# A decoder layer on one core: scores for the maxima from three of six pairs of parts in two halves of TensorE's rows, and cq and most of the down projection as plain float32 products

## The chip, the cores and the metric

The kernel runs on one core of a Trainium2 chip. The core has a matrix engine (TensorE, PE in the profile, with its weight loads as PEld), three engines for element-wise work (VectorE or DVE, ScalarE or ACT, GpSimd or POOL), a queue that issues DMAs (SyncE, SP), on-chip memory of 128 partitions (SBUF), and eight accumulator banks that TensorE writes (PSUM). The metric is the device time of one execution in microseconds; the time of a kernel is the median of its runs.

## The reference

One pre-norm decoder layer on 64 sequences of 128 tokens with 256 features, all in float32:

```python
x = x + attn(layernorm(x), W_attn, b_attn, W_proj, b_proj, bias_table)  # 16 heads of 16, causal, T5 bias
x = x + xattn(layernorm(x), ctx, ctx, mask, Wq, Wk, Wv, Wo)             # 16 heads of 16, keys masked
x = x + ffn(layernorm(x), w_gate, w_up, w_down)                         # 256 -> 704 -> 256
```

Attention is softmax(q k / 4 + bias) v. In the feed-forward part, both operands of each of the three products are first rounded, block by block of 16 values, to a 4-bit floating grid and scaled back; `h = silu(gate) * up`, rounded again, is multiplied by the rounded `w_down`. The rounding makes the result sensitive to small errors, so the products before it are made at float32 accuracy.

## The kernel before

Two sequences make a group; 32 groups go through the layer. Every step of a group has a name, such as `a0.sa2` (self-attention, sequence 0 of the group, second product of scores for heads 8 to 11) or `f1.dn` (feed-forward, sequence 1, down projection). `a` is self-attention, `c` cross-attention, `d` and `f` are the layer norms ahead of cross-attention and feed-forward. A list written out by hand, `ORDER`, gives every step a place and a stage. The steps of a group with stage s are issued s rounds of the list later, so that parts of six or seven groups are interleaved, and each engine works through its own instructions in that order. `SETUP` places the preparation of weights and bias tables among the first groups' steps, `BANKS` says which of the eight PSUM banks a step uses, `BUFS` how many buffers a tile name has.

How float32 accuracy is had from TensorE:

- *Split products* (`dense`, float32r operands): an operand is held as a high part (ScalarE, `high`) and the rest (VectorE, `low`). Three matmuls, high x high, high x low, low x high, make one product.
- *Plain products* (`plain`, float32 operands): one matmul, which appears in the trace as two passes.
- *Three bfloat16 parts*: queries and keys are cut into three parts (`Heads.part`, `take`, `rest`, `mid`, `low`). They are stored to DRAM (`store`) and loaded back (`Attention.load`) with rows = (part, dimension) and heads side by side, so that 96 rows hold six pairs of parts: q's parts (0,1,2), (0,1), (0) against k's parts in reverse order.

Attention for one sequence: `scores` (`sa`) makes q k for four heads at a time, a matmul of 96 rows each, `maxima` (`mx`, VectorE) adds bias or mask and takes each row's maximum, `tm`, `tw`, `tl` transpose the negated maxima and cut them into two bfloat16 parts, `bc` (`spread_max`) writes these by two DMAs into rows 96 and 97 of the loaded queries, whose partner rows in the keys hold ones. `scores_t` (`sb`) makes the transposed scores from 98 rows, so that the maximum is already subtracted; `ex` takes the exponential, `ph` and `pl` cut it into two float16 parts, `av` multiplies with the values, `cb`, `rv`, `cm` sum and normalise, `yt`, `yh`, `po`, `ad` project and add to x.

`cq` (queries of cross-attention) is a split product from `Norm.T` of kind d, whose low half VectorE makes (`d.lo`, L379). The down projection (`Feed.down`, L734) has six blocks of the 704 hidden features: five of 128 as split products, 15 matmuls, and the last 64 with high and low in the two halves of one tile, `hE`, two matmuls. Its operand `hT` is copied from a transposition by ScalarE (`turn_high`) and its low half is made by VectorE (`turn_low`, L722, L726).

Loading (L518) issues three DMAs, of 48, 32 and 16 rows of 4 KB. On SP the order in one round is:

```
mg  c0.lk  a0.bc  c1.lk  cq.st0  ck.st0  c0.lq  ck.st1  a1.bc  cq.st1  out  xg  c1.lq  cg
c0.bc  aq.st0  aq.st1  c1.bc  ak.st0  ak.st1  a0.lq  a0.lk  a1.lk  a1.lq
```

Of the kernel before, what the change touches and what calls it, by code (L numbers as in the profile page):

```python
# [9 lines left out]
F32 = mybir.dt.float32  # L10
F32R = mybir.dt.float32r
# [7 lines left out]
P = 128  # L19
# [23 lines left out]
    f0.am1:5 a0.mx1:2 a0.sa3:2 c1.ph1:4 d.lo:3 f1.rd2:6 c0.rv1:4 c1.av0:4 a0.mx3:2 a.ln:1 a0.sa2:2 ck.p0:2  # L43
    c0.cm1:4 c0.yh0:4 mg:3 a0.mx2:2 cq.mm:3 a1.sa0:2 ck.n1:2 cq.p0:3 c1.rv0:4 c1.cb0:4 f0.am2:5 c1.pl1:4
    c0.yt1:4 c0.yh1:4 a0.tm:2 c1.cm0:4 c1.av1:4 f1.ml0:6 cq.n1:3 c0.po:4 c1.yt0:4 a0.tw:2 ck.p1:2 c1.cb1:4
    f0.am3:5 ck.n2:2 c1.rv1:4 a0.tl:2 cq.p1:3 c1.cm1:4 a1.sa1:2 c1.yt1:4 a1.mx0:2 a1.mx1:2 c1.yh0:4 c0.lk:3
    ck.p2:2 c1.yh1:4 cq.n2:3 cq.p2:3 c0.ad:4 a0.bc:2 c1.lk:3 a0.sd0:2 c1.po:4 c1.ad:4 a0.sd1:2 f1.ml1:6 cq.st0:3
    f1.t0:6 f1.hi0:6 f.bn:4 f.ag:4 ck.st0:2 nm:3 f.ep:4 f0.xn0:5 c0.lq:3 f0.rd0:5 a1.sa2:2 f1.t1:6 f1.hi1:6
    a0.sb0:2 a0.ex0:2 a0.sb1:2 a0.ex1:2 a1.sa3:2 f1.lo0:6 f1.g1:5 f.pow:4 a0.sd2:2 cv.mm:2 f0.rd1:5 a0.sb2:2
    ck.st1:2 f.sh:4 a0.ph0:2 f1.lo1:6 f.ln:4 a.tp:1 f1.g0:5 a1.mx2:2 cv.p0:2 a1.mx3:2 f0.rd2:5 a.hi:1 f1.th0:5  # L50
    x.am0:4 x.am1:4 a.lo:1 cv.n1:2 f1.gt0:5 a0.pl0:2 a0.sd3:2 a1.tm:2 f1.dn:6 a0.sb3:2 x.am4:4 a1.tw:2 f1.th1:5
    f0.ml0:5 cv.p1:2 x.am2:4 x.am3:4 x.xn0:4 a1.tl:2 f1.gt1:5 c0.sa0:3 a0.ex2:2 c0.sa1:3 f1.ad:6 cv.n2:2 f1.u0:5
    a0.ex3:2 f1.u1:5 f0.ml1:5 c0.mx0:3 c0.mx1:3 a1.sd0:2 a1.bc:2 a1.sb0:2 cq.st1:3 a1.sd1:2 f1.bo0:5 x.rd0:4
    f1.bo1:5 x.rd1:4 a1.sb1:2 f1.am0:5 c0.sa2:3 a0.ph1:2 cv.p2:2 a1.ex0:2 f0.t0:5 c0.sa3:3 c0.mx2:3 out:6
    aq.mm:1 xg:0 c0.mx3:3 a1.sd3:2 x.rd2:4 f1.am1:5 a1.ex1:2 a0.pl1:2 f0.hi0:5 a1.sd2:2 f0.lo0:5 aq.p0:1 c1.lq:3
    f1.am2:5 a1.sb3:2 a0.av0:2 f0.t1:5 f0.hi1:5 a1.sb2:2 f0.lo1:5 cg:1 c0.tm:3 a1.ph0:2 a0.cb0:2 a0.rv0:2 aq.r:1
    c0.tw:3 a1.ex2:2 a0.cm0:2 f0.dn:5 c0.tl:3 a0.av1:2 aq.p1:1 a0.cb1:2 c1.sa2:3 a0.rv1:2 c1.sa0:3 x.ml0:4
    a1.pl0:2 a0.yt0:2 a1.ex3:2 f0.ad:5 a0.cm1:2 a0.yh0:2 ak.mm:1 c1.mx0:3 a0.yt1:2 c1.sa3:3 c1.mx2:3 c0.bc:3
    c1.sa1:3 a1.av0:2 c1.mx3:3 c0.sb0:3 f1.am3:5 a1.ph1:2 x.ml1:4 c0.sb1:3 ak.p0:1 a1.rv0:2 f.tp:4 aq.p2:1
    ak.r:1 a0.yh1:2 c0.ex0:3 a0.po:2 c0.ex1:3 c0.sb2:3 f.hi:4 a1.pl1:2 c1.mx1:3 f.lo:4 a1.cb0:2 aq.st0:1 ak.p1:1  # L60
    c0.sb3:3 a1.av1:2 aq.st1:1 a1.cb1:2 c1.tm:3 a1.rv1:2 av.mm:1 c0.ph0:3 c1.tw:3 a1.cm0:2 c0.ex2:3 a1.cm1:2
    f1.xn0:5 c1.tl:3 c1.bc:3 ak.p2:1 c0.ex3:3 ak.st0:1 a1.yt0:2 a1.yh0:2 a1.yt1:2 a1.yh1:2 c0.ph1:3 a.bn:0
    f0.g0:4 a.ag:0 a1.po:2 a0.ad:2 av.p0:1 f1.rd0:5 f0.th0:4 f0.g1:4 a1.ad:2 ak.st1:1 av.n1:1 d.bn:2 f0.gt0:4
    a0.lq:1 c0.pl0:3 a0.lk:1 c0.av0:3 c0.cb0:3 av.p1:1 c1.sb0:3 c0.pl1:3 a1.lk:1 c1.sb1:3 av.n2:1 f0.th1:4
    d.ag:2 f0.u0:4 a1.lq:1 a.ep:0 d.ep:2 f1.rd1:5 d.pow:2 c0.rv0:3 f0.gt1:4 c0.cm0:3 f0.u1:4 f0.bo0:4 c0.av1:3
    d.sh:2 c1.ex0:3 c1.ex1:3 c1.sb2:3 a.pow:0 av.p2:1 c1.sb3:3 a0.sa0:1 a0.sa1:1 c1.ph0:3 a.sh:0 f0.bo1:4 d.ln:2
    d.tp:2 c0.cb1:3 f0.am0:4 c1.ex2:3 a0.mx0:1 c0.yt0:3 c1.ex3:3 c1.pl0:3 d.hi:2 ck.mm:1
# [3 lines left out]
    wq1.ld:-1 wk1.ld:-1 wq1.sc:-1 wv1.ld:-1 wq1.hi:-1 b.ld:-1 wq1.lo:-1 wv1.hi:-1 wv1.lo:-1 w00.ld:-1 wk1.hi:-1  # L71
    wk1.lo:-1 w00.am0:-1 w00.am1:-1 w00.am2:-1 w00.xn0:-1 w10.ld:-1 w10.am0:-1 w10.am1:-1 w00.xe0:-1 b.li:-1
    w10.am2:-1 w00.rd0:-1 w00.rd1:-1 w10.xn0:-1 w00.rd2:-1 w00.ml0:-1 w00.ml1:-1 w10.xe0:-1 w00.t0:-1 w01.ld:-1
    w10.rd0:-1 w10.rd1:-1 w10.rd2:-1 w01.am0:-1 w10.ml0:-1 w10.ml1:-1 w01.am1:-1 w01.am2:-1 w01.xn0:-1 w10.t0:-1
    w01.xe0:-1 w01.rd0:-1 w01.rd1:-1 w11.ld:-1 w01.rd2:-1 w01.ml0:-1 w11.am0:-1 w01.ml1:-1 w01.t0:-1 w02.ld:-1
    w11.am1:-1 w11.am2:-1 w11.xn0:-1 w11.xe0:-1 w11.rd0:-1 w11.rd1:-1 w11.rd2:-1 b.lc:-1 w02.am0:-1 w02.am1:-1
    w11.ml0:-1 w02.am2:-1 w11.ml1:-1 w02.xn0:-1 w11.t0:-1 w02.xe0:-1 w02.rd0:-1 w02.rd1:-1 w12.ld:-1 w02.rd2:-1
    w02.ml0:-1 w12.am0:-1 w02.ml1:-1 w02.t0:-1 w12.am1:-1 w12.am2:-1 w12.xn0:-1 w12.xe0:-1 w03.ld:-1 w12.rd0:-1
    w12.rd1:-1 w12.rd2:-1 w12.ml0:-1 w03.am0:-1 w12.ml1:-1 b.st:-1 w03.am1:-1 w03.am2:-1 w03.xn0:-1 w03.xe0:-1
    w03.rd0:-1 w12.t0:-1 b.rv6:-1 w02.hi0:-1 b.lf:-1 b.fl6:-1 w10.hi0:-1 w03.rd1:-1 w03.rd2:-1 b.bh6:-1 b.rv3:-1  # L80
    b.rv2:-1 wv2.ld:-1 w13.ld:-1 w00.hi0:61 w03.ml0:61 w13.am0:61 b.rv5:83 w03.ml1:124 o.ld:145 w02.lo0:149
    w01.hi0:154 w00.lo0:166 w11.hi0:178 w13.am1:178 wp1.ld:193 w13.am2:193 w13.xn0:217 wk2.ld:221 w03.t0:304
    w03.hi0:310 wq2.ld:310 w10.lo0:310 w01.lo0:312 w21.ld:346 w13.xe0:360 w13.rd0:364 o.mm:414 b.rv1:414
    b.rv7:419 w21.am0:419 w21.am1:422 o.ad:439 b.rv0:439 w12.hi0:443 w13.rd1:443 b.fl3:456 w13.rd2:456
    w13.ml0:470 o.hi:501 wq2.sc:505 w11.lo0:507 w03.lo0:507 w13.ml1:524 w21.am2:532 b.fl5:543 w13.t0:543
    b.fl0:555 w21.xn0:556 b.bh0:561 b.bh5:565 b.bh3:568 b.fl2:569 w12.lo0:571 w13.hi0:571 w21.xe0:571
    w13.lo0:572 w21.rd0:572 w21.rd1:572 b.fl1:572 w21.rd2:577 b.bh2:600 b.bh1:614 wq2.hi:623 b.rv4:627 b.fl4:638
    w20.ld:642 w20.am0:650 b.bh4:652 b.fl7:652 b.bh7:658 w20.am1:669 w20.am2:682 w21.ml0:687 wo2.ld:687
    wq2.lo:687 w20.xn0:687 o.lo:773 w21.ml1:774 w20.xe0:774 w20.rd0:776 w20.rd1:902 w20.rd2:983 w21.t1:990
    w21.hi1:992 w21.lo1:1091 w21.t0:1290 w21.hi0:1304 w20.ml0:1307 w21.lo0:1307 w20.ml1:1307 w20.t1:1590  # L90
    w20.hi1:1611 w20.t0:1624 w20.lo1:1624 w20.hi0:1636 w20.lo0:1644
# [3 lines left out]
    a.tp:f1 aq.mm:f1 ak.mm:sa1 av.mm:sb0 ck.mm:yp cv.mm:f0 a0.sa0:sb0 a0.sa1:sa0 a0.sa2:sa0 a0.sa3:f0 a0.av0:yp  # L95
    a0.av1:sb1 a1.sa0:sa1 a1.sa1:sa0 a1.sa2:yp a1.sa3:pm a1.av0:sa0 a1.av1:sa1 d.tp:sa1 cq.mm:sb1 c0.sa0:sa0
    c0.sa1:f1 c0.sa2:sb1 c0.sa3:sa0 c0.sb0:f0 c0.sb1:f1 c0.sb2:f0 c0.sb3:f1 c0.av0:pm c0.av1:f1 c1.sa0:f1
    c1.sa1:sb0 c1.sa2:pm c1.sa3:yp c1.sb0:sa1 c1.sb1:yp c1.sb2:yp c1.sb3:f0 c1.av0:sb0 c1.av1:pm f.tp:pm
    f0.g0:f0 f0.u0:f0 f0.g1:sa0 f0.u1:sb1 f0.t0:pm f0.t1:sb1 f0.dn:sb0 f1.g0:sa0 f1.u0:pm f1.g1:sb1 f1.u1:sb0
    f1.t0:sb0 f1.t1:f1 f1.dn:sb0 b.li:yp b.fl0:f1 b.fl1:yp b.fl2:sa0 b.fl3:sb1 b.fl4:pm b.fl5:pm b.fl6:yp  # L100
    b.fl7:sb1 o.mm:pm w00.t0:f1 w10.t0:sa1 w01.t0:pm w11.t0:sb0 w02.t0:sa0 w12.t0:f0 w03.t0:yp w13.t0:yp
    w20.t0:sb0 w20.t1:f0 w21.t0:sb0 w21.t1:sb0 a0.sd0:sa1 a0.sd1:sa0 a0.sd2:sa1 a0.sd3:yp a1.sd0:sa1 a1.sd1:yp
# [4 lines left out]
    "hf": 2, "am": 2, "rc": 2, "xn": 2, "st": 2, "lna": 1, "lnd": 1, "lnf": 1, "xT": 2, "xTf": 1, "parts": 2, "rest": 1,  # L107
    "dd": 8, "neg": 2, "junk": 4, "twoT": 2, "pr": 2, "ph": 2, "pl": 2, "y": 2, "yT": 2, "xg": 6,
    "cg": 1, "mg": 1, "nm": 2, "hT": 1, "hE": 1, "ln": 2,
# [6 lines left out]
NROW = 6 * DK  # L116
# [4 lines left out]
def kernel(  # L121
# [20 lines left out]
    def bank(name):  # L142
        return psum.tile([P, 512], F32, tag=BANKS[step[0]], name=name)
# [77 lines left out]
    wgu = const.tile([P, 2, 2, 2, FF], F32R, name="wgu")  # L221


    wd = const.tile([P, 2, NKD, C], F32R, name="wd")
# [10 lines left out]
    for i in range(NST):  # L235
        qst.append(const.tile([P, H, T], BF16, name=f"qst{i}"))
        kst.append(const.tile([P, H, T], BF16, name=f"kst{i}"))
        nc.gpsimd.memset(kst[i][NROW : NROW + 2], 1.0)
# [89 lines left out]
    class Norm:  # L328
# [44 lines left out]
        def high(self):  # L373
            tag = "xTf" if self.kind == "f" else "xT"
            self.T = act.tile([P, 2, 2, GT], F32R, tag=tag, bufs=BUFS[tag], name=f"xT_{self.nm}")
            nc.scalar.copy(self.T[:, 0], self.tp)
# [123 lines left out]
    class Attention:  # L500
# [6 lines left out]
        def load(self, which):  # L507
            slot = count[which] % NST
            count[which] += 1
            src = self.g.heads[self.kind + which].dd[self.b].rearrange("a (d h) k -> (a d) (h k)", h=H)  # L510
            if which == "q":
                st = self.q = qst[slot]
            else:
# [564 lines left out]
```

## Time and profile before

| | |
|---|---|
| median of 3 runs | 1599.64 us (1596.57 to 1602.95) |
| profiled execution, its own time | 1603.48 us |
| its span, first to last instruction | 1601.7 us |
| TensorE busy | 1452.8 us, 91% of the span, 15298 matmuls |
| VectorE busy | 1448.0 us, 90%, 7263 instructions |
| ScalarE busy | 1310.4 us, 82%, 2765 instructions |
| GpSimd busy | 1274.0 us, 80%, 844 instructions |
| DMA | 191.07 MB, mean 119 GB/s |

A group of instructions in the profile is written as line, engine, operation, out<-in, shape, count, then busy time, mean duration of one in ns, idle time in front of it and what ended that. In a timeline a row is start, duration, engine, line, operation and count. Matmuls are pipelined: a record lasts longer than the distance to the next one, so that the pace of TensorE is read from starts.

### The profile page before, as it was taken

Reading aid. Unit: us, or ns where it says so; the run is one execution under the profiler, and the core shown is the slowest. Engines: PE = TensorE matmul, PEld = TensorE weight load, DVE = VectorE, ACT = ScalarE, POOL = GpSimd, SP = SyncE. Lnnn points to the kernel's source line nnn. Section 1 sums busy time; section 2 is a strip of 40 time slices with the busy share of each in tenths; the row PEclk is TensorE's granted clock in tenths of the full one; section 3 lists DMA queues with packets and bytes.
Section 4 is the critical chain, followed back from the end, with each engine's and each line's share of the span. In section 5 each row is a group of like instructions: output and inputs, shape, how many; then the busy total and the mean of one; then the engine's idle time right before and its main releaser. Section 6 shows DMA issues by size and latency. Waiting matters only on the chain.

```text
span 1601.7 us, 45513 instructions
## 1 busy us (share of the span) xinstructions
PE 1452.8 (91%) x15298; PEld 1296.4 (81%) x15298; DVE 1448.0 (90%) x7263; ACT 1310.4 (82%) x2765; POOL 1274.0 (80%) x844
## 2 busy tenths in 40 slices
PE   1468899999999999999999999999999999999875
PEld 0256788888889988889888889888899898898665
DVE  5656799999999999999999999999999999999873
ACT  0368888898899999989889989888899899898541
POOL 5444677888888988888898888888889888888864
PEclk9988999999999999999999999999999999999988
DMA  2544455555554455545555445555555554555200
GB/s 61 135 123 118 120 133 133 121 132 130 123 143 117 121 130 134 143 120 130 130 125 141 123 117 132 134 135 122 126 136 131 128 124 117 133 137 127 64 8 14
DMA packets 289834, 191.07 MB, mean 119 GB/s; under 512 B 224143, under 2 KB 264719, under 8 KB 289600
## 3 DMA queue, kind: packets, MB, share of 16 engines
q1 hardware_dynamic: 289600, 188.15, 47.6%
q8 instruction: 122, 2.00, 0.6%
q14 instruction: 112, 0.92, 0.2%
HBM read 128.26 MB, written 58.75 MB: 117 GB/s over the span
## 4 chain that ended last, share of the span: by engine, by line
PE 62%; DVE 15%; DMA 8%; ACT 7%; POOL 3%; SPq 3%; issue 3%; POOLq 0%; DVEq 0%; ACTq 0%
PE dp L734 6%; PE gp L320 6%; PE yp_c L326 4%; PE pp_ck L326 4%; DMA kst<-dd_ak 4%; DVE junk_c L540 4%; PE up L320 3%; PE sa_a L526 3%; PE vp_cv L326 3%; PE pp_cq L320 3%; PE sb_a L578 3%; PE yp_a L326 2%; PE yp_c L606 2%; PE sb_c L578 2%; PE sa_c L526 2%
## 5 line engine op out<-in xcount | busy, mean ns | idle before, releaser
L596 POOL TENSOR_TENSOR pl_c<-pr_c,ph_c 128x1024 f16<-128x1024 f32 x128 | 278.0, 2179 | 52.2 <-POOL rs_a L352 17.6
L596 POOL TENSOR_TENSOR pl_a<-pr_a,ph_a 128x1024 f16<-128x1024 f32 x128 | 274.8, 2147 | 28.9 <-ACT ph_a L592 25.8
L540 DVE CUSTOM_DVE_ANT_0 junk_a<-sa_a,bias_q 128x128 bf16<-128x128 f32 x1024 | 229.9, 283 | 26.8 <-PE sa_a L526 23.6
L540 DVE CUSTOM_DVE_ANT_0 junk_c<-sa_c,nm 128x128 bf16<-128x128 f32 x1024 | 225.3, 285 | 4.8 <-PE sa_c L526 3.6
L578 PEld LDWEIGHTS <-kst 98*128 98x128 bf16 x2048 | 144.9, 98 | 62.3 <-issue 13.4
L587 ACT ACTIVATE pr_c<-sb_c,lift 128x512 f32<-128x512 f32 x256 | 160.7, 678 | 25.3 <-PE sb_c L578 25.3
L526 PEld LDWEIGHTS <-qst 96*128 96x128 bf16 x2048 | 135.2, 98 | 45.8 <-issue 29.3
L587 ACT ACTIVATE pr_a<-sb_a,lift 128x512 f32<-128x512 f32 x256 | 168.2, 681 | 0.3
L320 PE MATMUL gp<-wgu,xT_f 128*128 128x352 f32 x768 | 154.1, 337 | 1.9 <-ACT pr_c L587 1.1
L565 ACT COPY sb_a<-bias_k 128x512 f32<-128x512 f32 x256 | 148.8, 601 | 0.0
L734 PE MATMUL dp<-wd,hT 128*128 128x256 f32 x960 | 139.1, 295 | 3.9 <-DVE am_h L286 2.5
L320 PE MATMUL up<-wgu,xT_f 128*128 128x352 f32 x768 | 139.3, 330 | 1.1 <-DVE xg L738 0.9
L592 ACT CAST ph_c<-pr_c 128x1024 f16<-128x1024 f32 x128 | 135.3, 1057 | 0.1
L592 ACT CAST ph_a<-pr_a 128x1024 f16<-128x1024 f32 x128 | 134.6, 1052 | 0.0
L734 PEld LDWEIGHTS dp<-wd,hT 128*128 128x128 f32 x960 | 123.1, 195 | 10.5 <-DVE hT L722 3.8
L308 POOL TENSOR_TENSOR xn_h<-xn_h,st_h 128x704 f32<-128x704 f32 x64 | 107.8, 1685 | 25.4 <-DVE sh_f L357 18.6
L320 PEld LDWEIGHTS gp<-wgu,xT_f 128*128 128x128 f32 x768 | 123.5, 191 | 3.4 <-ACT pr_c L587 1.3
L320 PEld LDWEIGHTS up<-wgu,xT_f 128*128 128x128 f32 x768 | 122.0, 188 | 3.5 <-DVE xg L738 1.2
L526 PE MATMUL sa_a<-kst,qst 96*128 96x128 bf16 x1024 | 95.1, 221 | 23.5 <-DMA kst<-dd_ak 19.9
L310 POOL TENSOR_TENSOR xn_h<-xn_h,st_h 128x704 f32<-128x704 f32 x64 | 108.3, 1693 | 0.4
L572 PE MATMUL sb_c<-ident_b,nm 128*128 128x512 bf16 x256 | 97.5, 381 | 5.0 <-DVE xg L647 4.6
L578 PE MATMUL sb_c<-qst,kst 98*128 98x128 bf16 x1024 | 99.3, 219 | 2.7 <-DMA qst<-twoT_c 2.7
(198 smaller groups left out, 4822.1 us busy)
## 6 DMA issues: line engine op xcount, KB each, us to landing
dd_aq<-parts_aq SPq DMA_DIRECT2D x64, 192.0 KB
dd_ak<-parts_ak SPq DMA_DIRECT2D x64, 192.0 KB
qst<-dd_aq SPq DMA_DIRECT2D x64, 192.0 KB
kst<-dd_ak SPq DMA_DIRECT2D x64, 192.0 KB
dd_ck<-parts_ck SPq DMA_DIRECT2D x64, 192.0 KB
kst<-dd_ck SPq DMA_DIRECT2D x64, 192.0 KB
dd_cq<-parts_cq SPq DMA_DIRECT2D x64, 192.0 KB
qst<-dd_cq SPq DMA_DIRECT2D x64, 192.0 KB
```

What stands on the lines that cost most here:

```text
L308: (nc.gpsimd if nm[0] in RDP else nc.vector).tensor_tensor(self.xn, self.xn, self.st, ALU.add)
L310: nc.gpsimd.tensor_tensor(self.xn, self.xn, self.st, ALU.subtract)
L320: nc.tensor.matmul(dst, lhs(a, i), rhs(b, i), start=(first and n == 0), stop=(last and n == 3 * nk - 1), skip_group_check=True)
L326: nc.tensor.matmul(dst, lhs(i), rhs(i), start=(first and i == 0), stop=(last and i == nk - 1), skip_group_check=True)
L526: nc.tensor.matmul(self.sa[:, r], self.q[:NROW, h], self.k[:NROW, h], start=(r == 0), stop=(r == HB - 1), skip_group_check=True,)
L540: nc.vector.tensor_tensor_reduce(junk[:, r], sa[:, r], bias_q[:, h] if self.kind == "a" else self.g.mask[:, self.b], op0=ALU.add, op1=ALU.max,
L565: nc.scalar.copy(self.sb[g], bias_k[:, g * HB : (g + 1) * HB])
L578: nc.tensor.matmul(self.sb[g][:, r], self.k[: NROW + 2, h], self.q[: NROW + 2, h], start=False, stop=(r == HB - 1), skip_group_check=True,)
L587: nc.scalar.activation(self.pr[o][:, g % 2 * HB : (g % 2 + 1) * HB], self.sb[g], AF.Exp, bias=lift)
L592: nc.scalar.copy(self.ph[o], self.pr[o])
L596: nc.gpsimd.tensor_tensor(self.pl[o], self.pr[o], self.ph[o], ALU.subtract)
L734: nc.tensor.matmul(self.po, l, r, start=(n == 0), stop=(n == len(terms) - 1))
```

## The change

- `scores` uses only the three leading pairs of parts: q's parts (0, 1), (0) against k's parts (1, 0), (0) in reverse order, 48 rows instead of 96. Heads 0 to 7 have these rows at partitions 64 to 111, heads 8 to 15 at 0 to 47; the other three pairs lie in the other half. One call (`sa0`, `sa1`) makes eight heads, alternating between the halves, each half into a bank of its own. Two calls take the place of four. The exponent's scores (`sb`) still use all six pairs, over 112 rows: the two rows of the maximum are now 48 and 49, and rows 32 to 63 that hold nothing else are cleared in q and set to one in k, once, by eight GpSimd instructions (before: four, of two rows).
- A load is six DMAs: for each half of the heads 32, 16 and 48 rows of 2 KB.
- `cq` is a plain product; `d.lo` goes, `wq2` is no longer split.
- Five of six blocks of the down projection are plain products; `lo0` goes and `lo1` keeps the last block's half. `wd` is held once, in float32. The memory that this frees goes to a second buffer of `hT` and of `cg`.
- `ORDER`, `SETUP` and `BANKS` are new lists. The stages are nearly the same. In the setup all steps of the eighth weight but one stand ahead of the first group's first step. On SP the order in one round is now:

```
a1.lq  a1.lk  a0.bc  ck.st0  cq.st0  c0.lk  cq.st1  c0.lq  a1.bc  c1.lq  cg  ck.st1  c1.lk  c0.bc
out  aq.st0  xg  aq.st1  mg  c1.bc  ak.st0  a0.lq  a0.lk  ak.st1
```

```diff
-        nc.gpsimd.memset(kst[i][NROW : NROW + 2], 1.0)
+        nc.gpsimd.memset(qst[i][32:HALF], 0.0)
+        nc.gpsimd.memset(kst[i][32:HALF], 1.0)
...
-                if self.kind == "ck":
+                if self.kind[0] == "c":
                     plain(
...
-            row = 0
-            for n in (3, 2, 1):
-                dst = st[row : row + n * DK].rearrange("r h k -> r (h k)")
-                nc.sync.dma_start(dst, src[: n * DK] if which == "q" else src[(3 - n) * DK :])
-                row += n * DK
+            for half in range(2):
+                hs = slice(half * (H // 2), (half + 1) * (H // 2))
+                row = (1 - half) * HALF
+                for n, r in ((2, row), (1, row + 2 * DK), (3, half * HALF)):
+                    nc.sync.dma_start(st[r : r + n * DK, hs], src[: n * DK, hs] if which == "q" else src[(3 - n) * DK :, hs])
...
-            for r in range(HB):
-                h = g * HB + r
-                nc.tensor.matmul(
-                    self.sa[:, r], self.q[:NROW, h], self.k[:NROW, h], start=(r == 0),
...
+            for half in range(2):
+                g = 2 * half + i
+                self.sas[g] = bank(f"sa_{self.nm}_{g}", half == 1).rearrange("p (r k) -> p r k", r=HB)
             for r in range(HB):
+                for half in range(2):
+                    rows = slice((1 - half) * HALF, (1 - half) * HALF + NPAIR)
+                    h = (2 * half + i) * HB + r
+                    nc.tensor.matmul(
+                        self.sas[2 * half + i][:, r], self.q[rows, h], self.k[rows, h], start=(r == 0),
...
-                    self.sb[g][:, r], self.k[: NROW + 2, h], self.q[: NROW + 2, h],
+                    self.sb[g][:, r], self.k[:NROW, h], self.q[:NROW, h],
...
-                self.hT = ff.tile([P, 2, NKD - 1, T], F32R, tag="hT", bufs=BUFS["hT"], name=f"hT{self.nm}")
-                nc.scalar.copy(self.hT[:, 0, :4], tp.rearrange("p (k t) -> p k t", t=T))
+                self.hT = ff.tile([P, NKD - 1, T], F32, tag="hT", bufs=BUFS["hT"], name=f"hT{self.nm}")
+                nc.scalar.copy(self.hT[:, :4], tp.rearrange("p (k t) -> p k t", t=T))
...
-            terms = [(self.hT[:, a, i], wd[:, w, i]) for i in range(NKD - 1) for a, w in ((0, 0), (0, 1), (1, 0))]
-            terms += [(self.hE, wd[:, 0, NKD - 1]), (self.hE, wd[:, 1, NKD - 1])]
-            for n, (l, r) in enumerate(terms):
-                nc.tensor.matmul(self.po, l, r, start=(n == 0), stop=(n == len(terms) - 1))
+            plain(self.po, lambda i: self.hT[:, i], lambda i: wd[:, i], NKD - 1, last=False)
+            for w in range(2):
+                nc.tensor.matmul(self.po, self.hE, we[:, w], start=False, stop=(w == 1), skip_group_check=True)
```

## The prediction

> **What bounds the kernel now.** I read the page's slices first, then a table of windows over the steady part, then TensorE's timeline inside one group, then the DMA queue's timeline. The page's slice of TensorE:
>
> ```profile
> PE   1468899999999999999999999999999999999875
> ```
>
> The steady part is 32 of the 40 slices (32 x 40.04 us = 1281 us). The window from 300 to 1400 us (columns: length, busy us of PE, weight loads, DVE, ACT, POOL, granted clock, DMA share, GB/s):
>
> ```profile
> 300.00:1400.00 1100.00, 1077.40 (x11725) 976.97 (x11723) 1067.32 (x5509) 995.00 (x2100) 946.70 (x617) 1.00 0.52 128
> ```
>
> TensorE is busy 98%, VectorE 97%, ScalarE 90%, GpSimd 86%, at full clock. The period of a group is read from one store to the next, 852.36 - 807.43 = 44.9 us; over many groups it is 44.7. So 29 periods (1281 / 44.7) carry the run, and a period is what must change.
>
> ```profile
> 807.43 0.49 SPq L791 DMA_DIRECT2D out_dram<-xg  x1
> ...
> 852.36 0.49 SPq L791 DMA_DIRECT2D out_dram<-xg  x1
> ```
>
> A busy TensorE hides its pace, since records overlap; the pace is the start of the next call less the start of this one, over the number of matmuls:
>
> ```profile
> 800.60 1.89 PE L326 MATMUL vp_cv<-wv,cg 128*128 128x256 f32 x8
> 802.33 0.39 PE L578 MATMUL sb_a<-qst,kst 98*128 98x128 bf16 x4
> ...
> 803.96 0.41 PE L490 MATMUL vp_cv<-v_c,nident_b 128*128 128x256 bf16 x2
> 804.22 0.27 PE L548 MATMUL sa_a<-ident_r,neg_a 128*16 128x128 f32 x1
> 804.24 2.04 PE L734 MATMUL dp<-wd,hT 128*128 128x256 f32 x15
> ...
> 806.36 0.40 PE L578 MATMUL sb_a<-qst,kst 98*128 98x128 bf16 x4
> 806.60 0.61 PE L526 MATMUL sa_c<-kst,qst 96*128 96x128 bf16 x8
> 807.05 0.41 PE L490 MATMUL vp_cv<-v_c,nident_b 128*128 128x256 bf16 x2
> ...
> 810.54 1.67 PE L320 MATMUL pp_aq<-xT_a,wq 128*128 128x256 f32 x12
> 812.04 0.40 PE L578 MATMUL sb_a<-qst,kst 98*128 98x128 bf16 x4
> ```
>
> Plain float32, 256 columns: 1.73 / 8 = 0.216 us for one pass, two passes to a product. Split product: 1.50 / 12 = 0.125 each. A down projection: 806.36 - 804.24 = 2.12 for 17. A score matmul: 0.45 / 8 = 0.056, its weight load hidden. Every call of a period at its pace adds up to about 43 us, so TensorE really waits only about 1.7 us of 44.7; VectorE has 0.97 x 44.7 = 43.4 us to do. Two engines are the bound, TensorE by its queue, VectorE by its load.
>
> **The change, part by part, per period.**
>
> *Score products for the maxima.* 64 matmuls of 96 rows become 64 of 48 rows, alternately in rows 64 to 111 and 0 to 47. Before: 64 x 0.056 = 3.58. If the two halves run side by side, 32 pairs count. No row shows a pair. Lower end: a pair can't beat the 128 columns that one of them streams, 0.056. Upper end: no overlap, 0.112. Near the lower end stands the sums' row (L606), where matmuls of 49 columns follow each other every 0.025 (16 in 0.40 us, each with its own weight load): two could be issued in 0.051, so issue does not keep a pair from 0.056. I take 0.060: 1.92, a gain of 1.66.
>
> *Entering and leaving the half arrays.* 8 calls, 16 changes. The nearest row is the transposition of the maxima (L548), which holds 16 columns of the array only: the call before it takes 0.26 for two, and the down projection starts 0.02 behind it, as behind other calls. Lower end 0; upper end the time that a matmul stays in the array after the next could start, its 0.221 us record less 0.056 = 0.166. I take 0. The Trainium skill (TensorEngine Tiling (Array Packing), Key Properties) says that a change of tiling mode drains TensorE. The L548 row does not show it for column tiles, and no row here shows it for row tiles; by the rule, at 0.166 a change, 16 changes would be 2.7 us and turn the gain into a loss.
>
> *cq as plain float32.* 12 x 0.125 = 1.50 becomes 8 x 0.216 = 1.73: +0.2. *Down projection.* 17 products (2.12) become 5 plain ones and 2 split ones: 10 x 0.216 + 2 x 0.125 = 2.41, +0.3 each, +0.6 for two. TensorE in sum: -1.66 + 0.23 + 0.58 = -0.85.
>
> *VectorE.* The low halves go:
>
> ```profile
> L722 DVE TENSOR_TENSOR hT<-ht,hT 128x512 fp32r<-128x512 f32 x64 | 43.5, 680 | 6.8 <-ACT hT L713 6.8
> L379 DVE TENSOR_TENSOR xT_d<-tp_d,xT_d 128x512 fp32r<-128x512 f32 x32 | 22.0, 687 | 0.8 <-ACT xT_d L376 0.6
> ```
>
> With the fifth block's subtraction (L726, 16.5 us) 82 us in 32 groups, 2.6 a period: 43.4 becomes 40.8. TensorE stays the longest queue (43 - 0.85 = about 42.2), so this pays only through TensorE's waits, between 0 and all 1.7 of them. ScalarE's copies stay at 0.59; at 0.90 x 44.7 = 40.4 it is not yet the bound.
>
> *SP's queue.* Each load of q or k is 6 DMAs of 2 KB rows instead of 3 of 4 KB, the bytes the same: 24 more issues a period. An issue is 0.42 to 0.51:
>
> ```profile
> 824.75 2.08 SPq L454 DMA_DIRECT2D dd_ak<-parts_ak  x2
> 826.93 1.41 SPq L518 DMA_DIRECT2D qst<-dd_aq  x3
> 828.46 2.94 SPq L518 DMA_DIRECT2D kst<-dd_ak  x6
> ...
> 832.98 0.61 PE L526 MATMUL sa_a<-kst,qst 96*128 96x128 bf16 x8 [0.61 <-DMA kst<-dd_ak]
> ```
>
> SP then issues 69 times instead of 45, about 31 of 44 us. For element 0 of self-attention the new list issues one store, 6 + 6 loads: about 6 us against 5.1 (824.75 to 829.9), while it puts 15.6 us of TensorE work between ak's product and the first scores, against 14.2. The wait at 832.98 should shrink, by about 0.5. For element 1 the last load is issued about 12.3 us behind the first store, against 8.3; the list gives 2.0 us more work, and before those scores ran at 838.04, 1.9 us after the loads landed (the last was issued by 833.06; element 0's landed 3.1 after 829.9, at the wait's end): 4.0 later, 2.0 more work, 1.9 of cover, so nothing is left, and I count +0.2. c0's q load comes 1.8 us later, of about 2.8 us of cover. The two maxima rows (L559) wait behind these loads; between the transposition of the maxima and the first exponent scores the list leaves 3.5 us for a0, before 4.1.
>
> *TensorE's waits, 1.7.* A down projection no longer waits for VectorE's low half: 0.2 in one of two (813.20 to 815.52 is 2.32, not 2.12). Less 0.5 at 832.98, and 0.2 more for element 1. New: the list leaves 1.7 us between f.tp and f0.g0 where it left 4.0, and copy and subtraction (0.59 + 0.69, rows L376 and L379) behind a 0.17 us matmul latency take 1.45 with both queues free: 0 to 1.5, I take +0.4, about one instruction ahead of them on one queue. Sum -0.1.
>
> *Start.* GpSimd clears 8 stretches of 32 rows instead of 4 of 2, 1.8 us each (7.2 us for 4): +7.2 us, of which 5.4 were idle before the first weight's step at 14.84; and the eighth weight is finished ahead of the first layer norm. 0 to 8 us, I take +4.
>
> Sum: (-0.85 - 0.1) x 29 = -28, + 4 = -24. The profiled execution took 1603.5 us (span 1601.7 and 1.8 around it), 3.8 above the median of 1599.6: 1579.5 by it, **1576** as a median.
>
> **Rivals.**
>
> *VectorE was what TensorE waited for.* For it: 97% busy. Against it: the waits I can name end with DMA and ScalarE. Waits fall by 1.0 instead of 0.1: (-0.85 - 1.0) x 29 + 4 = -50, 1550.
>
> *The halves run one after the other.* The change then does not do what it says. For it: no row shows two matmuls in the array's halves, and the score matmuls run at one per 0.056. Scores stay at 3.6, plain products cost +0.8: (+0.8 - 0.1) x 29 + 4 = +24, 1624. The Trainium skill (TensorE: Matmul & The Clock Gate, Part 3) says that matmuls in distinct row groups run concurrently, about 4 ns apart; no run here shows it yet.
>
> *Each change of tile empties the array* (the other side). Place: 16 changes around L526's calls. At the upper end, 16 x 0.166 = 2.7: (-0.95 + 2.66) x 29 + 4 = +54, 1653; at half of it 1615. It decides where 16 changes eat the 24 us, at 24 / 29 / 16 = 0.052 us a change. Against it: L548.
>
> *Loads come late.* For it: SP at 31 of 44 us, no cover left for element 1. Against it: the list gives 2 us more there. If the 12 more issues of the burst took 0.51 instead of 0.42 and c0 lost as much, scores would wait about 1.3 more: (-0.95 + 1.3) x 29 + 4 = +14, 1614.
>
> **How the numbers follow.** Forecast 0.56, VectorE's relief 0.12, no overlap 0.12, emptied array 0.11, late loads 0.09. The forecast's own range, with a pair at 0.056 to 0.075 (-0.98 to -0.37) and waits from -0.9 to +0.3, not both at one end, is 1558 to 1598. Over all cases 1547 to 1635; beyond it lies an array emptied at nearly the full price. A run can tell about 0.5% (8 us) from no change. Faster: 0.51 of the forecast + 0.12 = 0.63. Same: 0.05 of the forecast, 0.02 of the emptied array, 0.03 of the late loads = 0.10. Slower: 0.27.
>
> **What the new profile would show.** Right: L542's eight matmuls take about 0.25 us to the next call (wrong at 0.45; emptied if the call behind starts 0.1 late); plain cq 1.73 and dn 2.41; VectorE near 93% with 41 us a period; a period of 43.8. Late loads would show as TensorE waiting on kst<-dd_ak or qst<-dd_cq more than 40 us in all. The prediction is wrong above all if a pair is not 0.06, or if the changed order, which I follow only at these places, makes a wait that I do not list.

## The result, and the profile after

The changed kernel takes 1643.1 us (median of 4 runs, 1642.6 to 1646.1) against 1599.9 us: a ratio of 1.027 with a 95% interval of 1.025 to 1.030. It is slower by 43 us; 24 us less was forecast. The profiled execution has a span of 1641.3 us. Two numbers split the difference, both from the stores of a group's result: the first one lies at 284.5 us instead of 272.3, and their distance in the steady part (from the fourth to the fourth from last) is 45.57 us instead of 44.40 by the same count. Of all executions behind this document one is left out, of 5182 us, in the first kernel of the experiments, whose other three agree within 0.4%; its trace is of that one, so that its waits are not read.

The steady part after, in the view of windows (length, then busy time of PE, weight loads, DVE, ACT and POOL):

```profile
300.00:1400.00 1100.00, 1080.43 (x11069) 916.93 (x11069) 1019.32 (x5221) 983.89 (x2037) 921.87 (x599) 1.00 0.51 125
```

VectorE fell from 97% to 92.7%, close to the 93% forecast. TensorE is still at 98%: it was not given the time that the score matmuls were to save. Its timeline around c0's first score call shows two things:

```profile
825.42 0.58 PE L741 MATMUL dp<-we,hE 128*128 128x256 f32 x2
825.93 0.23 PE L542 MATMUL sa_c<-kst,qst 48*128 48x128 bf16 x1
825.93 0.23 PE L542 MATMUL sa_c_second<-kst,qst 48*128 48x128 bf16 x1
826.00 0.22 PE L542 MATMUL sa_c<-kst,qst 48*128 48x128 bf16 x1
826.00 0.22 PE L542 MATMUL sa_c_second<-kst,qst 48*128 48x128 bf16 x1
...
826.11 0.22 PE L542 MATMUL sa_c_second<-kst,qst 48*128 48x128 bf16 x1
826.26 0.41 PE L501 MATMUL vp_cv<-v_c,nident_b 128*128 128x256 bf16 x2
```

The two halves start together, and pairs follow each other every 0.05 to 0.07 us: eight matmuls take 0.33 us to the next call (825.93 to 826.26), where they took 0.45. But the next call starts 0.15 us behind the last pair (826.11 to 826.26), though a matmul of this kind steps every 0.056, and 0.21 us pass from the last matmul of the down projection to the first pair (the median over 24 groups; 0.12 in the kernel of whole rows below).

The second part of the loss is further on. This is the chain of waits of the changed kernel from there to c0's transposition of the maxima (start, length, engine, what). TensorE carries the chain before and after; for 6.8 us VectorE does:

```profile
826.33 0.05 PE sa_c_second L542
826.37 0.28 DVE junk_c L554
...
828.14 0.34 DVE xg L745
828.48 0.05 DVE hf L714
828.53 0.29 issue
828.83 2.12 DVE st_x L311
830.95 0.20 DVE junk_c L554
...
833.08 0.04 issue
833.12 0.28 PE sa_c_second L562
```

TensorE's waits that this makes, from 300 to 1400 us (in total, times, longest; the weight load and the matmul of the same step, once a period), and the group of instructions that sticks out in the chain (busy us, mean ns):

```profile
PEld sa_c_second L562 <- DVE neg_c L554: 19.3, 24, 0.8
PE sa_c_second L562 <- DVE neg_c L554: 16.6, 24, 0.7
```

```profile
L311 DVE TENSOR_SCALAR st_x<-xn_x 128x512 int32<-128x512 int32 x32 | 58.6, 1831 | 0.0
L311 DVE TENSOR_SCALAR st_h<-xn_h 128x704 int32<-128x704 int32 x64 | 34.0, 531 | 3.3 <-POOL xn_h L302 3.3
```

`st_x` is the step `x.rd0`, a mask on 128 x 512 integers. It takes 1.83 us, while `st_h`, the same operation on 704 columns, takes 0.53. In the kernel before, the two rows were the other way about:

```profile
L304 DVE TENSOR_SCALAR st_h<-xn_h 128x704 int32<-128x704 int32 x64 | 61.9, 967 | 2.4 <-POOL xn_h L295 2.4
L304 DVE TENSOR_SCALAR st_x<-xn_x 128x512 int32<-128x512 int32 x32 | 16.3, 510 | 0.5 <-POOL xn_x L295 0.5
```

So the trace of before did show that this operation is sometimes held; a mean of 967 ns beside 510 for fewer columns asks for a look at what runs beside it.

### The profile page after: what moved, and what is told of

Read it like the earlier page. It is cut to its first block, busy times and chain, and to the rows that moved or that the text cites. A ratio compares the mean times of both kernels' runs of the same rounds, so it can differ in the third digit from the quotient of the medians.

```text
span 1641.3 us, 45574 instructions
## 1 busy us (share of the span) xinstructions
PE 1499.8 (91%) x14850; PEld 1255.4 (76%) x14850; DVE 1420.3 (87%) x7092; ACT 1332.1 (81%) x2764; POOL 1282.2 (78%) x848
## 4 chain that ended last, share of the span: by engine, by line
PE 74%; DVE 13%; POOL 3%; SPq 3%; ACT 2%; DMA 2%; issue 2%; POOLq 0%; ACTq 0%; DVEq 0%
PE dp L333 9%; PE gp L327 8%; DVE junk_c L554 6%; PE up L327 4%; PE yp_a L333 4%; PE sb_c L592 3%; DVE st_x L311 3%; PE sb_c L586 3%; PE vp_cv L333 3%; PE pp_cq L333 3%; PE pp_ck L333 3%; PE yp_c L620 3%; PE yp_c L333 3%; PE pp_ak L327 3%; PE sb_a L592 3%; PE vp_av L327 3%
## 5 line engine op out<-in xcount | busy, mean ns | idle before, releaser
L610 POOL TENSOR_TENSOR pl_c<-pr_c,ph_c 128x1024 f16<-128x1024 f32 x128 | 274.2, 2142 | 35.1 <-ACT ph_c L606 22.2
L601 ACT ACTIVATE pr_c<-sb_c,lift 128x512 f32<-128x512 f32 x256 | 166.5, 689 | 33.0 <-PE sb_c L592 31.1
L592 PEld LDWEIGHTS <-kst 112*128 112x128 bf16 x2048 | 148.5, 98 | 49.1 <-issue 7.3
L333 PE MATMUL dp<-wd,hT 128*128 128x256 f32 x640 | 158.5, 396 | 2.6 <-DVE am_h L293 1.2
L327 PE MATMUL up<-wgu,xT_f 128*128 128x352 f32 x768 | 144.1, 330 | 0.0
L554 DVE CUSTOM_DVE_ANT_0 junk_a<-sa_a,bias_q 128x128 bf16<-128x128 f32 x512 | 117.8, 287 | 26.4 <-PE sa_a L542 16.7
L554 DVE CUSTOM_DVE_ANT_0 junk_c<-sa_c,nm 128x128 bf16<-128x128 f32 x512 | 117.4, 284 | 25.2 <-PE sa_c_second L542 24.9
L554 DVE CUSTOM_DVE_ANT_0 junk_c<-sa_c_second,nm 128x128 bf16<-128x128 f32 x512 | 117.3, 284 | 0.0
L554 DVE CUSTOM_DVE_ANT_0 junk_a<-sa_a_second,bias_q 128x128 bf16<-128x128 f32 x512 | 112.7, 285 | 0.0
L315 POOL TENSOR_TENSOR xn_x<-xn_x,st_x 128x512 f32<-128x512 f32 x32 | 40.7, 1273 | 85.0 <-DVE st_x L313 85.0
L542 PEld LDWEIGHTS <-qst 48*128 48x128 bf16 x2048 | 62.6, 95 | 57.2 <-issue 24.7
```

The costliest lines, as they stand in the source:

```text
L315: (nc.gpsimd if nm[0] in RDP else nc.vector).tensor_tensor(self.xn, self.xn, self.st, ALU.add)
L327: nc.tensor.matmul(dst, lhs(a, i), rhs(b, i), start=(first and n == 0), stop=(last and n == 3 * nk - 1), skip_group_check=True)
L333: nc.tensor.matmul(dst, lhs(i), rhs(i), start=(first and i == 0), stop=(last and i == nk - 1), skip_group_check=True)
L542: nc.tensor.matmul(self.sas[2 * half + i][:, r], self.q[rows, h], self.k[rows, h], start=(r == 0), stop=(r == HB - 1), skip_group_check=True,)
L554: nc.vector.tensor_tensor_reduce(junk[:, r], sa[:, r], bias_q[:, h] if self.kind == "a" else self.g.mask[:, self.b], op0=ALU.add, op1=ALU.max,
L592: nc.tensor.matmul(self.sb[g][:, r], self.k[:NROW, h], self.q[:NROW, h], start=False, stop=(r == HB - 1), skip_group_check=True,)
```

## The experiments

Theory A: going into the half arrays and out of them costs TensorE time and eats what the pairs save. Rival B: it is free, and the loss comes from the new written lists. Rivals C and D are about the plain products. All ratios are to the kernel before, run on the same chip. Cuts of the written lists below show the steps in their order, not the lines of the file.

**Whole rows again.** The scores of the changed kernel use 96 rows and six pairs again, with three loads; lists, banks and plain products stay.

```diff
-                    rows = slice((1 - half) * HALF, (1 - half) * HALF + NPAIR)
+                    rows = slice(0, NROW)
```

> The changed kernel with its scores back on the whole array: 96 rows, six pairs, 16 matmuls of an attention one after the other, three loads of q and k each instead of six. The written lists, the banks and the plain float32 products stay as changed, so this tells what the two halves are worth by themselves. Theory A (every move into the half arrays and out of them costs TensorE about 0.095 us, 16 moves a period, so 1.5 us of the 1.66 us that the pairs save is spent again): the time stays within half a per cent of the changed kernel's 1643 us, about 1643 + 29 x 0.14 = 1647 us, and the period is about 46.1 us. Rival B (the moves are free, as the prediction had it, and the whole loss comes from the new lists and the plain products): 1643 + 29 x 1.66 = 1691 us, period 47.6 us. Both expect TensorE's waits for the maxima ahead of the two context transposes (22.6 + 26.1 us in all in the changed kernel) to be about as long here, if it is the list that makes them.

Measured: 1637.2 us (median of three), ratio 1.023 (1.020 to 1.025). B's 1691 is out: in this list the halves save nothing. The 1647 of A is 10 us off on the other side, so the halves cost something more than their moves, which a later run finds.

**The plain products alone**, in the lists of before (`cq` and five blocks of the down projection plain; four splitting steps out of the lists):

```diff
-            terms = [(self.hT[:, a, i], wd[:, w, i]) for i in range(NKD - 1) for a, w in ((0, 0), (0, 1), (1, 0))]
+            plain(self.po, lambda i: self.hT[:, i], lambda i: wd[:, i], NKD - 1, last=False)
```

> The kernel before with the plain float32 products of cq and of five of six parts of the down projection alone: scores, written order and banks are those of before, with the four splitting steps that the plain products don't need taken out. Theory A (the plain products cost TensorE what the prediction priced, 0.81 us a period, and the VectorE time they free is worth nothing): 1600 + 29 x 0.81 = 1623 us, period 45.5 us, cq about 1.73 us and a down projection about 2.41 us. Rival C (the plain products alone are the whole loss): 1643 us. Rival D (the freed 2.6 us of VectorE a period shortens waits by as much as TensorE pays): 1600 us or less.

Measured: 1612.7 us, ratio 1.0065 (1.0044 to 1.0086). From start to next start, cq's product takes 1.78 us instead of 1.51 and each of the two down projections 2.40 instead of 2.21, together 0.65 us a period. Behind the two transpositions of the maxima ahead of the down projections, the next matmul starts 0.11 us later where it was 0.03, another 0.15 in sum. But the period grows by 0.39 only: other calls of TensorE got shorter, those of c's exponent scores (sb_c) and of c's products with the values and its projection (yp_c) by 0.17 each. So A's 1623 is 10 us too high, and the plain products are about 10 of the 43 us. Neither C nor D holds.

**The halves one after the other.** In a score call the loops over heads and halves change places:

```diff
-            for r in range(HB):
-                for half in range(2):
+            for half in range(2):
+                for r in range(HB):
```

> The changed kernel with the eight matmuls of a score call in another order: the four of one half of the rows, then the four of the other, instead of turn and turn about. Nothing else differs. If two neighbours run side by side only when their rows differ (what the trace's equal start times say), each call gets longer by about four paces of 0.058 us = 0.23 us, eight calls a period: +1.86 us a period, 1643 + 54 = 1697 us. If the halves gained nothing by the order (or each change from one half to the other cost something), the time stays at 1643 us or falls below it.

Measured: 1641.5 us, ratio 1.025 (1.023 to 1.027), the same as the changed kernel's. My expectation was wrong. TensorE's timeline of this kernel, whose queue holds four matmuls of `sa_a` and then four of `sa_a_second`:

```profile
811.53 0.23 PE L542 MATMUL sa_a<-kst,qst 48*128 48x128 bf16 x1
811.54 0.23 PE L542 MATMUL sa_a_second<-kst,qst 48*128 48x128 bf16 x1
811.60 0.22 PE L542 MATMUL sa_a<-kst,qst 48*128 48x128 bf16 x1
811.61 0.22 PE L542 MATMUL sa_a_second<-kst,qst 48*128 48x128 bf16 x1
```

The second half does not wait for its turn in the queue. The Trainium skill (TensorE: Matmul & The Clock Gate, Part 3) gives TensorE a window of 64 entries in which loads of weights for other rows are pulled ahead, which fits, and adds that matmuls themselves start strictly in the order of the queue; here the first of the second half starts before the second of the first half, so the measurement decides against that sentence.

**The moves by themselves.**

> A kernel that computes nothing of the reference (its output is zeros): TensorE alone runs eleven stretches of 20 rounds each, with 40 fp32r products ahead of each stretch, nothing to wait for. A round is a row of score matmuls and four or eight fp32r products of 256 columns: (1) 4 products; (2) 8 whole-row matmuls + 4 products; (3) 16 + 8; (4) 8 matmuls in turn on the two halves + 4 products; (5) 16 + 8; (6) as 4 with the halves one after the other; (7) as 4 on one half alone; (8) 4 matmuls of 16 columns + 4 products; (9) 8 + 8; (10) 8 half matmuls + 8 whole-row ones; (11) 16 + 16. Twice a short round less the long one is the cost of going into the form and out of it, with no pace assumed. Theory A: 0.19 us for the halves (4, 5), also next to bf16 matmuls of the whole rows (10, 11), and 0 for the whole rows (2, 3). Rival B: 0 for the halves too. For 16 columns (8, 9) I expect 0, as the waits of the transposes show no such gap. The halves in turn come at 0.058 us a pair, one after the other at about 0.058 us a matmul.

Start to start, medians of 20 rounds in us; the last column is twice the short round less the long one:

| a round | short: 8 matmuls + what follows | long: twice as many of both | twice short - long |
|---|---|---|---|
| whole rows | 0.431 + 0.562 | 0.877 + 1.036 | 0.073 |
| halves in turn | 0.327 + 0.670 | 0.551 + 1.147 | 0.296 |
| halves and whole-row bf16 | 0.330 + 0.553 | 0.553 + 1.000 | 0.213 |
| 16 columns, float32 (4 matmuls) | 0.978 + 0.669 | 1.851 + 1.149 | 0.294 |

The timeline has a whole-row round and a half-row round of it:

```profile
24.85 0.62 PE L58 MATMUL full<-kb,qb 96*128 96x128 bf16 x8
25.28 0.72 PE L54 MATMUL prod<-w 128*128 128x256 f32 x4
25.84 0.62 PE L58 MATMUL full<-kb,qb 96*128 96x128 bf16 x8
...
92.67 0.40 PE L64 MATMUL half<-kb,qb 48*128 48x128 bf16 x8
93.00 0.74 PE L54 MATMUL prod<-w 128*128 128x256 f32 x4
93.67 0.40 PE L64 MATMUL half<-kb,qb 48*128 48x128 bf16 x8
```

A round takes 0.99 us with whole rows (24.85 to 25.84) and 1.00 with halves (92.67 to 93.67). Going in and out costs 0.296 - 0.073 = 0.22 us, 0.11 a move (0.670 - 0.562 on the way in), and 0.213 / 2 = 0.11 next to bf16; eight matmuls at 0.056 a pair save 0.22. At eight matmuls a call the gain is spent to the last hundredth; at 16 it is 0.21 (1.70 against 1.91). Theory A stands. The 16 columns show the same sum, against my expectation, though I have no whole-array row of that float32 form to take off. The halves in two blocks took 0.338, in turn 0.327, eight on one half 0.547.

**Two gaps closed, and maxima moved up.** Beside the changed kernel (1644.2 us, ratio 1.0279, 1.0255 to 1.0304) I ran three written orders. The first leaves out four of the 16 moves:

```diff
-    a0.sa0:2 d.tp:3 a.sh:1 f1.am1:5 a0.mx0:2 a0.sa1:2
+    a0.sa0:2 a.sh:1 f1.am1:5 a0.mx0:2 a0.sa1:2 d.tp:3
...
-    c0.sa0:3 a1.bc:2
+    c0.sa0:3 c0.sa1:3 a1.bc:2
...
-    a1.ex0:2 c0.sa1:3 f1.u1:5
+    a1.ex0:2 f1.u1:5
```

> The changed kernel once more, as the base of the three kernels run beside it: 1643 us, ratio 1.027.

> The changed kernel with two of the eight gaps between score calls closed: the transposes of the norm (d.tp) go behind a0's second score call instead of between the two, and c0's second score call comes straight behind its first. No operation is added or taken away; four of the 16 moves between the half arrays and the whole go. Theory A: 2 x 0.19 us a period, 29 x 0.38 = 11 us less, 1632 us. Rival B (moves are free): 1643 us, or more if c0's call now waits for its banks.

Measured: 1646.2 us, ratio 1.0287 (1.0265 to 1.031), no gain. From start to next start, the score calls and what stands ahead of them (sa_a, sa_c, tp_d, sb_a, vp_cv) lost 0.45 us a period, as A says, and pp_aq and the second half of cq's parts took 0.32 and 0.14 more: the wait for VectorE, now partly on the bank of a0's sum (last row; 0.2 in the changed kernel), had grown by most of what was saved.

```profile
PEld sa_c_second L560 <- DVE neg_c L552: 19.7, 24, 0.8
PE sa_c_second L560 <- DVE neg_c L552: 17.1, 24, 0.7
...
PE yp_a L618 <- DVE neg_c L552: 9.0, 23, 0.4
```

> The changed kernel with four maxima moved up in the written order: c0's and c1's second pair of maxima come straight behind the score call that they read, ahead of the activation's two products and the quantising's two rounding steps (c0) and ahead of the split of aq (c1). If the 22.6 + 26.1 us that TensorE waits for these maxima ahead of the two transposes are on the path that sets the period, up to 0.9 us a period goes: 1643 - 27 = 1616 us, and these two rows of the waits shrink to a few us. If VectorE's 42.6 busy us of 45.9 bind by themselves, the wait moves to what was passed over (the waits of GpSimd for the rounding steps, 85 us in all, or of TensorE for hf) and the time stays within half a per cent of 1643 us.

The edit was `c0.mx1 c0.mx3` behind `c0.sa1`, and `c1.mx1 c1.mx3` behind `c1.sa1`. Measured: 1680.7 us, ratio 1.051, slower by 36 us than the base. The rows of neg_c are gone, and others have come:

```profile
ACT parts_ak L455 <- DVE rest_ak L449: 46.3, 23, 2.0
...
DVE junk_c L552 <- PE sa_c_second L540: 42.6, 49, 1.8
...
PE sb_c L584 <- DVE rest_ak L449: 34.0, 23, 1.5
```

c1's maxima now stood at the head of VectorE's queue before their scores were made, and ak's subtraction, whose bank c0's exponent scores need next, waited behind them. The edit mixed two places. c0's part had worked: `x.rd0` now comes behind c0's maxima, and `st_x` takes 0.47 us in the mean instead of 1.8. That c1's place alone made the loss is read from these rows; no run moved it alone.

> The two edits together: the closed gaps and the early maxima. If they are independent, 1643 - 11 - 27 = 1605 us; if the waits move elsewhere, about 1632 us.

Measured: 1674.5 us, ratio 1.046: the same fault, with 6 us less than the run before it.

**c0's place alone.**

```diff
-    f1.bo0:5 x.rd0:4 a0.pl1:2 a1.sb1:2 f0.t0:5 c0.mx1:3 cv.p2:2 aq.mm:1 f1.bo1:5 c0.mx3:3 x.rd1:4
+    f1.bo0:5 c0.mx1:3 c0.mx3:3 a0.pl1:2 a1.sb1:2 f0.t0:5 cv.p2:2 aq.mm:1 f1.bo1:5 x.rd0:4 x.rd1:4
```

> The changed kernel with three steps of VectorE moved in the written order, around c0 alone: c0's second pair of maxima (mx1, mx3) comes behind the first of f1's two products (f1.bo0), and the first rounding step of the quantising (x.rd0, 2.1 us on VectorE with what it waits for) behind the second one (f1.bo1). In the changed kernel's chain VectorE carries the path for 6.8 us a period here, from the last of c0's first eight score matmuls (826.33) to c0's transpose (833.12), and TensorE stands idle for 0.69 us of it. If that wait is on the path that sets the period, the row of TensorE's wait for neg_c goes to nearly nothing and the time falls by up to 29 x 0.69 = 20 us, to 1623 us. If the rounding step that is put off (GpSimd waits 69 to 85 us for it already) or VectorE's load as such binds next, the time stays within half a per cent of 1643 us; if it starves f0's and f1's next products, it grows, as it did by 35 us when c1's maxima passed the split of ak.

Measured: 1611.4 us, ratio 1.0061 (1.0038 to 1.0083): 33 us, more than the 20 of the wait's row. The call a0.av ahead of the transposition, which holds that wait, is 0.83 us a period shorter, and ht and pp_aq ahead of it 0.39: TensorE had been late for VectorE in three calls, not one.

> The same, with the two gaps between score calls closed (d.tp behind a0's second call, c0's second call straight behind its first). Closing them alone took 0.45 us a period from TensorE's score calls and their neighbours, and c0's wait for VectorE grew by 0.46 us. Theory A: with VectorE's stretch around c0 shortened the 0.45 us come to light: 29 x 0.45 = 13 us below the kernel with the early maxima alone, about 1610 us. Rival B (moves between the halves and the whole cost nothing): the same time as that kernel.

Measured: 1606.0 us, ratio 1.0029 (1.0012 to 1.0045), 5 us below instead of 13. The four moves show as time now, but not all of it: the period is 0.20 us shorter, and the first store of the profiled execution comes 5 us later (286.5 against 281.1).

> The same three steps moved in the kernel whose scores use the whole rows. Theory: the wait of c0's transpose belongs to the written order and not to the halves, so the kernel of whole rows has it too and gains by the same edit: 1639 - 20 = 1619 us. A call of eight whole-row matmuls with the products behind it takes 0.43 + 0.56 us and one of eight half-row matmuls 0.33 + 0.67 us, so this kernel and the one with the halves and the early maxima should agree within half a per cent. If the wait comes from the halves, nothing changes here: 1639 us.

Measured: 1595.9 us, ratio 0.9965 (0.9952 to 0.9979): faster than both kernels. The wait belongs to the list, as expected, but the two forms do not agree: whole rows are 15 us below the halves. TensorE is busy without a gap here:

```profile
300.00:1400.00 1100.00, 1100.00 (x11416) 984.47 (x11414) 1013.19 (x5385) 1010.68 (x2101) 950.73 (x618) 1.00 0.51 130
```

**What the halves still cost.** The last kernel, its three loads of q and of k each cut in two by heads:

```diff
-                nc.sync.dma_start(dst, src[: n * DK] if which == "q" else src[(3 - n) * DK :])
+                for half in range(2):
+                    hs = slice(half * (H // 2), (half + 1) * (H // 2))
+                    nc.sync.dma_start(st[row : row + n * DK, hs], src[: n * DK, hs] if which == "q" else src[(3 - n) * DK :, hs])
```

> The kernel of whole rows with the early maxima (1596 us), in which each of the three loads of q and of k is cut in two by heads, so that six of half the width are issued, as the halves need them; the same bytes land in the same places. It tells apart what the halves still cost, 15 us against this kernel: their first output comes 7 us later (281 against 274 us) and their period is 0.17 us longer. If the number of loads makes the late start and a part of the period, this kernel's first output is at about 280 us and its time is 1603 to 1611 us. If the loads are hidden and the score calls themselves (moves in and out) make the difference, it stays at 1596 us.

Measured: 1623.0 us, ratio 1.0149 (1.0129 to 1.0168), 27 us for loads that move the same bytes: the first store comes at 287.1 us instead of 274.2 and the period is 0.62 us longer. The largest waits of SP's queue, with three loads and then with six:

```profile
SPq L568 <- ACT parts_ck L424: 152.5, 24, 7.5
SPq L568 <- ACT hE L727: 111.2, 25, 4.5
SPq L568 <- ACT xT_a L382: 75.3, 25, 3.5
```

```profile
SPq L460 <- POOL parts_aq L455: 57.9, 24, 2.6
SPq L569 <- ACT twoT_c L562: 51.2, 24, 3.0
SPq L569 <- ACT parts_ck L424: 40.9, 25, 2.3
```

With three, SP stands idle for over 7 us at one place of a period; with six nothing is above 3.0, and what it issues comes later: c0's first score call takes 0.73 us in the mean instead of 0.46, a1's 0.62 instead of 0.44. With as many loads the kernel with halves (1611 us) is faster than this one; but its scores use only the first five of the six, and these all of them, so what the loads cost the halves is not measured by itself.

> The kernel of whole rows with the early maxima, with the down projection split into three fp32r products again (its high parts in two buffers, its low part in one; the two splitting steps of VectorE stand behind the copies as before; cq stays a plain product). TensorE is busy without a break in the kernel it comes from (1100.00 us of 1100), so its 0.58 us a period, the price of the plain form, should come off: 1596 - 29 x 0.58 = 1579 us. If the 1.7 us that the split gives back to VectorE (from 40.9 to 42.6 us a period of 43.7) bring back waits like that of c0, the time is 1590 to 1600 us or more.

To make room, this kernel also has one buffer instead of four for what the maxima write (`junk`). Measured: 1693.3 us, ratio 1.059, a miss, and it doesn't answer its question. The split's steps hold f0's bank until VectorE has read it, and the next transposition, into the same bank, waits for them:

```profile
PEld ht L716 <- issue: 41.6, 23, 2.1
PE ht L716 <- DVE hL L732: 38.2, 23, 1.9
```

In this list both of f0's transpositions use one bank, which the plain form frees with ScalarE's copy alone. The row is 1.7 us of the 3.0 by which the period grew; the rest was not traced. What the plain products are worth under the new list stays open.

**One step.** Of the three steps moved around c0, `x.rd0` alone:

```diff
-    f1.bo0:5 x.rd0:4 a0.pl1:2
+    f1.bo0:5 a0.pl1:2
...
-    f1.bo1:5 c0.mx3:3 x.rd1:4
+    f1.bo1:5 c0.mx3:3 x.rd0:4 x.rd1:4
```

> The changed kernel with one step of the written order moved: the first rounding step of the quantising (x.rd0, an int32 instruction of VectorE from SBUF to SBUF) goes behind c0's last maxima (c0.mx3) instead of ahead of the second pair; the maxima stay where the change put them. In the changed kernel this instruction starts while GpSimd works on pl_a (2.14 us) and ends 0.28 us behind that, in all of its instances that start so: it takes 1.83 us in the mean, 0.42 us where GpSimd does nothing long. If this hold is the whole cause of the stretch around c0, this one step brings what the three moved steps brought: 1611 us, ratio 1.006, and TensorE's wait for neg_c goes. If the place of the maxima matters by itself, only the hold's part goes: 1644 - 29 x 0.7 = 1624 us or more.

Measured: 1609.4 us, ratio 1.0054 (1.0036 to 1.0073): all of it, 35 us for one step of the list. The maxima's place was not the cause. The row of `st_x` in this kernel:

```profile
L309 DVE TENSOR_SCALAR st_x<-xn_x 128x512 int32<-128x512 int32 x32 | 13.8, 432 | 0.0
```

And this is what held it in the changed kernel, in the timeline of GpSimd and VectorE:

```profile
828.53 2.14 POOL L610 TENSOR_TENSOR pl_a<-pr_a,ph_a 128x1024 f16<-128x1024 f32 x1
828.83 2.12 DVE L311 TENSOR_SCALAR st_x<-xn_x 128x512 int32<-128x512 int32 x1
```

GpSimd's instruction ends at 830.67, VectorE's at 830.95. In the changed kernel 29 of the 32 `st_x` start while a long GpSimd instruction runs, and all 29 end 0.28 us behind it (0.277 to 0.287); the other three take 0.42. In the kernel before, 29 of the 64 `st_h` were held by `pl_c`: 24 end 0.38 us behind it, five stand through the next instruction too and take 3.35 us. Not every VectorE instruction is held: in the changed kernel c0's maxima (`junk_c`), which read PSUM, take 0.29 us beside `pl_a` and `pl_c` and away from them. The Trainium skill (SBUF — State Buffer, SBUF: two separate sides) says that VectorE and GpSimd share a pair of ports, which some VectorE instructions need, `tensor_scalar` among those that can, and that the one that starts first holds it for its whole instruction while the other is blocked. These rows agree with it, with 1.4 us in the mean as the price of one meeting here (1.83 against 0.43). The step moved in this run took those 1.83 us ahead of the second pair of maxima; 0.43 of them are its own time, and no run parts the two.

## Why the prediction was wrong

The 43 us, from these runs and in this order: plain products +10 (1.0065); the new list with whole rows and `x.rd0` out of GpSimd's way -16 against that (1.0065 to 0.9965); the halves with their loads +14 (1609.4 against 1595.9), of which about 10 lie in the first store (284.9 us against 274.2) and the rest in the period (44.42 against 44.28); `x.rd0` in GpSimd's way +35 (1644.2 against 1609.4). The parts depend on the order: with `x.rd0` in the way the halves cost 6 us (1643.1 against 1637.2).

- *TensorE's waits* is the step that failed most: -0.1 us a period in the forecast. What was listed did no harm: the waits of a0's scores for their loads are gone, though they were worth 0.35 us a period and not 0.5 (8.6 us in 12 waits between 300 and 1400 us; the one at 832.98 was taken for every period), and TensorE's waits show no row for f0.g0, where +0.4 was put. What was not listed is 1.2 us at c0 (45.65 against 44.42 a period), from one step of the list that is neither in the diff's code nor on TensorE. I had followed the new list at the places where a load or a copy was near, and not VectorE's queue between the first scores of an attention and the transposition of its maxima. The forecast named an unlisted wait of the changed order as what would make it wrong.
- *Entering and leaving the half arrays*, taken as 0 with an upper end of 0.166: 0.11 a move, 16 moves, 1.8 us. I trusted the row of the 16-column transposition (L548), which is not a row of this form, and whose own form shows 0.29 us for in and out where it runs without other waits. I had also read it at places where a split product follows, 0.02 to 0.03 us behind; at the fourth place of a period the trace of before has 0.11:

```profile
838.61 0.27 PE L548 MATMUL sa_a<-ident_r,neg_a 128*16 128x128 f32 x1
838.72 0.19 PE L606 MATMUL yp_c<-v_c,ph_c 128*128 128x49 bf16 x1
```

  So the row could not speak for 0. The prediction's own sign, the call behind starting 0.1 late, is what the timeline shows: 0.15 behind the last pair instead of 0.056. The rival's break-even, 0.052 a move, was right in kind: beyond it the halves bring nothing. The rule that a change of form drains TensorE, set aside there, was the better guide.
- *Score products*: right, a pair takes 0.056 (0.060 taken, -1.66; at 0.056 it is -1.8). The rival that the halves run one after the other is out.
- *cq and down projection*: +0.81 priced, with 0.2 back from the wait for the low half; 0.65 measured, and 0.15 behind the transpositions, which was not priced.
- *Start*: +4, 12.2 measured (10.9 in the second profiled execution), and by another cause. The kernel of whole rows with six loads has its first store at 287.1 us although it clears only four stretches; with three loads it is 274.2. It is mostly the loads, not GpSimd's clearing.
- *Loads come late*, 0.09, was partly true: not as waits of over 40 us on one row, but as 0.12 to 0.23 us a period inside two score calls (means of 0.39 us each in the first profiled execution, 0.43 and 0.46 in the second; undisturbed 0.33) and in the start.
- *VectorE*: 92.7% as forecast, which is luck, since it is of a longer period: 42.2 us and not 41. The steps that went were 82 us of the page, but VectorE's total fell by 28 only (1448.0 to 1420.3): `st_x` alone took 42 more (58.6 against 16.3) while `st_h` took 28 less, and the rest I didn't trace. That freed VectorE time doesn't pay for the plain products was right: alone they made the kernel slower, though by half of their price.

## What to carry to other kernels

Small tiles of the array pay only by the run: 16 moves at 0.11 us cancelled 32 pairs at 0.056, so score calls of two halves want 16 matmuls or more between changes of form, or neighbours in the same form. Before pricing the arithmetic of a change that comes with a new written order, walk each engine's new queue between a product and its consumer, and look for any instruction whose mean differs between shapes or places without a reason: one held instruction weighed more (35 us) than the plain products and the halves together (24). Loads that are cut finer are not free when one queue issues all of them, even at the same bytes.

## What the runs showed of the hardware that I had not expected

- Matmuls for different halves of the rows overlap even if the queue holds them in two blocks of four: 0.338 us for eight, 0.327 in turn, 0.547 on one half.
- A change between whole array and half arrays costs 0.11 us each way, next to fp32r and next to bf16 calls.
- A VectorE instruction on 512 integers a partition, SBUF to SBUF, stands still while GpSimd works on a long one and ends 0.28 us behind it: 0.42 us alone, 2.1 us beside a GpSimd instruction of 2.14 us. VectorE's maxima, which read PSUM, take 0.29 us either way.
- Twice as many loads of q and k for the same bytes cost 27 us of 1596 where SP issues all of them, 13 of them before the first store.
